# New places for GpSimd's products and TensorE's sums in a selective-scan schedule

## The chip, the core and the metric

The kernel runs on one core of a Trainium2 chip. The metric is the device time in microseconds of one execution. A core has TensorE (PE), VectorE (DVE), ScalarE (ACT), GpSimd (POOL) and SyncE (SP), which here issues the DMAs. Each engine works through its own queue in program order and waits where an instruction needs what another engine has not yet done.

## The reference

Four image-like tensors of 64 x 64 positions and 96 channels pass four layers. Only the first one matters here: a projection to 192 channels, a 3 x 3 convolution, and a selective scan over 4096 positions that is made in four directions (row order and column order, each forward and backward). Cut to the scan:

```python
def step(h, inp):
    u_t, dt_t, B_t, C_t = inp
    dA = jnp.exp(dt_t[..., None] * A)
    h = dA * h + (dt_t * u_t)[..., None] * B_t[:, None, :]
    y = jnp.sum(h * C_t[:, None, :], axis=-1)
    return (h, y)
_, ys = jax.lax.scan(step, h0, (uT, dT, BT, CT))
```

The state has 16 entries a channel. Layer 1 is a convolution, layers 2 and 3 are attention, a Fourier filter and two feed-forward networks with layer norms.

## The kernel before

**Tiles.** 8 channels x 16 states fill the 128 partitions, so the 192 channels make `NG` = 24 groups an image, and the 4 images 96 units. A unit is scanned in two **phases**: an even one in row order ("row") and an odd one in column order ("column"). That makes N = 192 phases. The 4096 positions of a phase are cut into four chunks, q = 0 to 3, of `CH` = 1024.

**Steps.** The loop at L1950 runs 8 steps a phase. Step k = 0 to 3 makes the forward scan of chunk q = k (L1970), which starts from the last column of the chunk before. Step k = 4 to 7 makes the backward scan of chunk q = 7 - k (L1977), which starts from `edge`, the first column of the chunk behind it. VectorE makes all of them. ACT makes the decays exp(dt * A) into PSUM (`decay`, tile `pa`, L1669 and L1675), two PSUM tiles in turn.

**From state to y.** y is the sum over states of h * C. GpSimd multiplies the states by C in place (`times_c`, L1658; C is the tile `rep`), and TensorE sums over the states into the PSUM tile `py` (`reduce`, L1691). Mostly the backward state is added to the forward one first (L1988, VectorE), so that one product serves both. For the chunks in `apart[n]` the backward scan writes over B instead (tile `B` in a row phase, `Bc` in a column one, noted in `gs`), and forward and backward are multiplied and summed each for itself. There is one such chunk, q = 3, while `"pre"` is not in `done`; after that there are two, q = 3 and 2.

**Other work of a phase.** `times_b` (L1653, GpSimd) makes B times dt * u of the next unit in place. `copy_b` (L1628, ACT) copies it into column order for the odd phase. `load_delta`, `load_du` and `load_rep` issue loads on SP. `result` (L1698, ACT) empties `py`, and `store_result` (L1705) issues 16 stores. The forward states lie in five buffers, S0 to S4, that `places` hands out: the scan of chunk 1 takes the buffer of chunk 2 of the phase before, chunk 2 that of chunk 3, chunk 3 that of chunk 1.

**Order.** The scan part runs under a manual schedule, which keeps the order in which the program issues. `plan(n)` enters actions for steps t + k, with t = 8 n, into a table, by `at`. In a step the loop issues first a decay, then the actions of the table, then the scan and what belongs to it, and last `pieces`.

**Side work.** `pieces` fits in what the other layers need: before all scans are fed, the convolution and projections of images 1 to 3 (`before_scans`); then layers 1 to 3 of the images that have been scanned (`rest`). A piece has a cost for each of PE, ACT, POOL, DVE and DMA, in this order. Each step adds the row `gains[step % 16]` to five credits, which are held to `cap`, and pieces run while the credits last. One piece of a convolution block, `LONG`, is allowed only at step 12 of 16. When images 1 to 3 have been through the convolution, `"pre"` is set. What is not done after the last scan is run without shares, and image 3 passes its layers alone in the tail.

Of the kernel before, what the change touches and what calls it, by code (L numbers as in the profile page):

```python
# [73 lines left out]
def layers(ctx: ExitStack, tc: tile.TileContext, a: dict, out):  # L74
# [37 lines left out]
    late = []  # L112
# [22 lines left out]
    done = {}  # L135
# [1446 lines left out]
    def phase(n):  # L1582

        b, g = units[n // 2]
        return b, g, n % 2
# [130 lines left out]
    class Lane:  # L1716
# [32 lines left out]
    credit = [0.0] * 5  # L1749

    gains = [
        (2.8, 1.2, 0.4, 0.8, 1.6), (2.8, 1.2, 0.4, 0.8, 1.6),
        (2.8, 0.2, 0.4, 0.8, 1.6), (2.8, 0.4, 2.2, 0.8, 1.6),
        (2.8, 1.2, 0, 0.8, 1.6), (2.8, 1.4, 0.4, 0.8, 1.6),
        (3.2, 1.0, 1.2, 1, 1.8), (3.2, 2.4, 1.4, 1, 1.8),
        (2.8, 1.4, 0.4, 0.8, 1.6), (2.8, 1.4, 0.4, 0.8, 1.6),
        (2.8, 1.4, 0.4, 0.8, 1.6), (2.8, 2.4, 0.6, 0.8, 1.6),
        (2.8, 2.8, 0.6, 0.8, 1.6), (2.8, 1.4, 0.6, 0.8, 1.6),
        (3.2, 2.4, 0.8, 1, 1.8), (3.2, 2.4, 1.4, 1, 1.8),
    ]  # L1760
    cap = (4.4, 3.0, 3.2, 1.6, 4.0)

    def pieces(step):

        clock[0] += 1
        assert clock[0] % 16 == (step + 1) % 16
        for free, bank in returned:
            free.append(bank)
        returned.clear()
        for e in range(5):  # L1770

            more = 1.25 if e in (2, 4) and clock[0] > 8 * (N - NG) else 1
            credit[e] = min(cap[e], credit[e] + gains[step][e] * more)
        for lane in list(lanes):
            if not lane.live():
                lanes.remove(lane)
                continue
            for s in list(lane.streams):
                while s[1] is not None:
                    if s[1] == NEXT:  # L1780
                        if s[2] == clock[0]:
                            break
                        lane.advance(s)
                        continue
                    if s[1] == LONG:
                        if step != 12:
                            break
                        cost = (0, 5.0, 0, 0)
                    else:
                        cost = s[1]  # L1790
                        if any(
                            c > 0 and credit[e] < min(c, cap[e]) - 0.5 for e, c in enumerate(cost)
                        ):
                            break
                    for e in range(len(cost)):
                        credit[e] -= cost[e]
                    lane.advance(s)
                if s[1] is None:
                    lane.streams.remove(s)
# [88 lines left out]
    def at(step, f, *args):  # L1888
        acts.setdefault(step, []).append((f, args))

    def plan(n):

        t, u = 8 * n, n // 2
        two = "pre" in done
        apart[n] = (3, 2) if two else (3,)
        row = n % 2 == 0
        b, g, _ = phase(n)
        last, first = g == NG - 1, g == 0

        if row:  # L1900
            for q, k in ((0, 7), (1, 8), (2, 9), (3, 10)):
                at(t + k, load_du, u + 1, q)
            for q, k in ((0, 3), (1, 5), (2, 15), (3, 16)):
                at(t + k, load_delta, u + 1, q)
            if last:
                for q in range(NCH):
                    at(t + 2 + q, load_rep, b + 1, 0, q)
                for q, k in ((3, 8), (2, 9), (1, 11), (0, 12)):
                    at(t + k, load_rep, b + 1, 1, q)
            for q, k in ((2, 2), (3, 3), (1, 4), (0, 6)):  # L1910
                at(t + k, copy_b, u, q)
            if first:
                for q in range(NCH):
                    at(t + 6 + q // 2, copy_rep, b, q)
        else:
            for q, k in ((0, 2), (1, 3), (2, 6), (3, 9)):
                at(t + k, times_b, u + 1, q)

        if two:
            at(t + 4, times_c, n, 2)  # L1920
            at(t + 5, times_c, n, 3)
            at(t + 6, times_c, n, 3, True)
            at(t + 7, times_c, n, 2, True)
            at(t + 6, reduce, n, 2)
            at(t + 7, reduce, n, 3)
            at(t + 8, reduce, n, 3, True)
            at(t + 8, reduce, n, 2, True)
        else:
            at(t + 4, times_c, n, 3)
            at(t + 6, times_c, n, 3, True)  # L1930
            at(t + 7, times_c, n, 2)
            at(t + 6, reduce, n, 3)
            at(t + 8, reduce, n, 3, True)
            at(t + 8, reduce, n, 2)
        late = 0 if row else 1
        at(t + 8, times_c, n, 1)
        at(t + 9 + late, times_c, n, 0)
        at(t + 10, reduce, n, 1)
        at(t + 10 + 2 * late, reduce, n, 0)
        if not row:  # L1940
            at(t + 13, result, u)
            for j in range(4):
                at(t + 14 + j, store_result, u, j)

    with tc.manual_schedule():
        ordered[0] = True
# [3 lines left out]
        for step in range(8 * N):  # L1950
            n, k = divmod(step, 8)
            if k == 0:
                plan(n)
                if n % (2 * NG) == 2 * NG - 2 and n // 2 + 1 < len(units):
                    b = units[n // 2 + 1][0]
                    assert done.get(("back", b)) == NBLK, (n, done)
# [10 lines left out]
            if k < 4:  # L1967
                q = k
# [5 lines left out]
            else:  # L1974
                q = 7 - k
# [8 lines left out]
                else:  # L1984
                    if q:
                        edge = big.tile([128, 1], F32, tag="edge", name="edge", bufs=2)
                        nc.vector.tensor_copy(edge, to[:, 0:1])
                    nc.vector.tensor_tensor(Ss[n, q], Ss[n, q], to, ALU.add)  # L1988
            pieces(step % 16)
            if n == N - 1 and k >= 4:  # L1990
                for i in (2 * k - 8, 2 * k - 7):
# [24 lines left out]
def kernel_body(tc: tile.TileContext, a: dict, out):  # L2016
    layers(tc, a, out)
# [117 lines left out]
```

## Time and profile before

| what | value |
|---|---|
| median of three runs | 5528.23 us (5521.36 to 5540.81) |
| the profiled execution, its time | 5537.81 us |
| the profiled execution, its span | 5536.0 us |

Busy time of the engines by stretch, in us:

| stretch, us | length | PE | DVE | ACT | POOL |
|---|---|---|---|---|---|
| 0 to 298, before the scans | 298 | 253 | 94 | 181 | 82 |
| 298 to 1775, one chunk apart | 1477 | 1192 | 1226 | 1101 | 1140 |
| 1775 to 5106, two chunks apart | 3331 | 2464 | 3094 | 2166 | 2710 |
| 5106 to 5536, tail | 430 | 349 | 204 | 118 | 42 |

A row of a group reads: line, engine, operation, out<-in by tile names, shapes and count, then the busy time in all and the mean of one in ns, then the engine's idle time just before them and what ended it. A row of a timeline has the start and the length in us first; "x2" means that two such instructions follow on each other in the row, and brackets hold the idle time before it and what ended it. A row of waits reads: the engine and the instruction that waited, what it waited for, the sum in us, how often, and the longest.

### The profile page before, as it was taken

The numbers are of one execution on the slowest core, as the hardware profiler recorded it, in microseconds if no ns is written. First come the engines' busy times: TensorE is split into PE (matmuls) and PEld (weight loads), VectorE is DVE, ScalarE is ACT, GpSimd is POOL, SyncE is SP. The second block draws the span as 40 slices with busy tenths as digits, with TensorE's granted clock in tenths as the row PEclk, the third lists the DMA queues.
The fourth block names the chain that finished last, engine by engine and source line by source line (L and its number), as shares of the span: only waits on it lengthen the run. The fifth ranks groups of instructions, "written<-read, shape, count | busy, mean of one in ns | idle before, by whom it ended". The sixth has DMA issues, their size and how long they took to land. (4 is left out here: it accounts for less than half of the span.)

```text
span 5536.0 us, 60837 instructions
## 1 busy us (share of the span) xinstructions
PE 4258.0 (77%) x20550; PEld 1581.5 (29%) x20550; DVE 4618.4 (83%) x3098; ACT 3566.0 (64%) x4554; POOL 3973.4 (72%) x1968
## 2 busy tenths in 40 slices
PE   7967888878886876777658876877578767786878
PEld 4422222222221221345102211542012213451346
DVE  4268888788889998999899999999898989998454
ACT  5667777777786568666865677576755676566133
POOL 1357877778778778878887788787987787787000
PEclk9977989888997986678668866787588768886888
DMA  4334444434456533455456434363565335563012
GB/s 125 91 110 115 126 114 117 135 105 124 117 162 175 163 99 89 128 160 156 125 145 173 117 87 119 115 200 103 147 170 146 97 99 165 161 176 96 17 55 96
DMA packets 298092, 694.68 MB, mean 125 GB/s; under 512 B 58184, under 2 KB 95156, under 8 KB 297652
## 3 DMA queue, kind: packets, MB, share of 16 engines
q1 hardware_dynamic: 297780, 690.80, 44.2%
q8 instruction: 162, 2.65, 0.2%
q14 instruction: 150, 1.23, 0.1%
HBM read 564.22 MB, written 126.35 MB: 125 GB/s over the span
## 5 line engine op out<-in xcount | busy, mean ns | idle before, releaser
L1658 POOL TENSOR_TENSOR S<-S,rep 128x1024 f32<-128x1024 f32 x768 | 1806.5, 2362 | 678.9 <-DVE S L1970 628.4
L1691 PE MATMUL py<-S,red 128*32 128x512 f32 x3072 | 956.8, 782 | 380.9 <-POOL S L1658 273.1
L1675 ACT ACTIVATE pa<-dl,nega 128x512 f32<-128x512 f32 x1152 | 792.9, 689 | 579.0 <-DVE Bc L1977 295.3
L1669 ACT ACTIVATE pa<-dl,nega 128x1024 f32<-128x1024 f32 x576 | 642.2, 1115 | 515.7 <-DVE S L1988 239.5
L1653 POOL TENSOR_TENSOR B<-B,rep 128x1024 f32<-128x1024 f32 x384 | 903.0, 2360 | 14.7 <-DMA B<-du_s 14.7
L1970 DVE TENSOR_TENSOR_SCAN S<-pa,S,Bc 128x1024 f32<-128x1024 f32 x288 | 676.3, 2348 | 230.8 <-PE py L1691 161.2
L1970 DVE TENSOR_TENSOR_SCAN S<-pa,S,B 128x1024 f32<-128x1024 f32 x288 | 675.8, 2347 | 134.0 <-PE py L1691 46.3
L1628 ACT COPY Bc<-B 128x1024 f32<-128x1024 f32 x384 | 741.0, 1982 | 0.0
L1988 DVE TENSOR_TENSOR S<-S,pa 128x1024 f32<-128x1024 f32 x439 | 533.7, 1216 | 6.6
L393 PE MATMUL p_conv<-low,conv_w 128*96 128x512 f32 x864 | 421.7, 639 | 32.0 <-ACT u L405 29.4
L1658 POOL TENSOR_TENSOR B<-B,rep 128x1024 f32<-128x1024 f32 x164 | 388.0, 2370 | 75.1 <-DVE pa L1977 38.8
L1977 DVE TENSOR_TENSOR_SCAN B<-pa,B 128x1024 f32<-128x1024 f32 x164 | 379.1, 2312 | 48.2 <-ACT Bc L1628 41.9
L1658 POOL TENSOR_TENSOR Bc<-Bc,rep 128x1024 f32<-128x1024 f32 x165 | 387.0, 2361 | 5.3 <-DVE pa L1977 4.0
L1977 DVE TENSOR_TENSOR_SCAN Bc<-pa,Bc 128x1024 f32<-128x1024 f32 x165 | 381.8, 2314 | 4.7
L1691 PEld LDWEIGHTS py<-S,red 128*32 128x32 f32 x3072 | 118.7, 121 | 908.9 <-POOL S L1658 518.0
L1234 POOL CAST h<-y 128x1536 fp8e5<-128x1536 f16 x64 | 95.5, 1492 | 312.7 <-ACT y L869 301.3
L1977 DVE TENSOR_TENSOR_SCAN pa<-pa,edge,B 128x1024 f32<-128x1024 f32 x124 | 291.5, 2350 | 2.8 <-ACT pa L1669 2.8
L1977 DVE TENSOR_TENSOR_SCAN pa<-pa,edge,Bc 128x1024 f32<-128x1024 f32 x123 | 289.2, 2351 | 5.2 <-ACT pa L1675 5.2
L1691 PE MATMUL py<-Bc,red 128*32 128x512 f32 x660 | 200.0, 787 | 95.1 <-POOL Bc L1658 95.1
L393 PE MATMUL p_conv<-high,conv_w 64*96 64x512 f32 (+1 forms) x576 | 265.0, 597 | 0.0
L1056 PE MATMUL p_mean<-t,centre 96*96 96x512 f32 x256 | 174.3, 792 | 110.7 <-ACT sq L1048 31.8
L1970 DVE TENSOR_TENSOR_SCAN S<-pa,B 128x1024 f32<-128x1024 f32 x96 | 218.9, 2280 | 23.3 <-ACT pa L1669 23.3
(274 smaller groups left out, 7411.4 us busy)
## 6 DMA issues: line engine op xcount, KB each, us to landing
dl<-delta_s SPq DMA_DIRECT2D x770, 256.0 KB
B<-du_s SPq DMA_DIRECT2D x768, 256.0 KB
z_s<-z SPq DMA_DIRECT2D x48, 512.0 KB
zl<-z_s SPq DMA_DIRECT2D x64, 384.0 KB
side<-y_s SPq DMA_DIRECT2D x112, 192.0 KB
rep<-bc_s SPq DMA_DIRECT2D x64, 256.0 KB
tw<-in_dft SPq DMA_DIRECT2D x64, 256.0 KB
side<-in_xT SPq DMA_DIRECT2D x64, 192.0 KB
```

The costliest lines, as they stand in the source:

```text
L393: nc.tensor.matmul(p, lhsT=conv_w[: src.shape[0], k, oc * C : (oc + 1) * C], rhs=src[:, ky : ky + RPB, kx : kx + HW], start=(k == 0), stop ...
L1056: nc.tensor.matmul(pm, lhsT=centre, rhs=t[:, blk(i)], start=True, stop=True)
L1234: nc.gpsimd.tensor_copy(h, y, saturate=False)
L1628: nc.scalar.copy(dst.rearrange("p (w h) -> p h w", h=HW)[:, q * h : (q + 1) * h, :], src.rearrange("p (h w) -> p h w", w=HW),)
L1653: nc.gpsimd.tensor_tensor(Bs[u, q], Bs[u, q], reps[units[u][0], 0, q], ALU.mult)
L1658: nc.gpsimd.tensor_tensor(t, t, c_of(n, q), ALU.mult)
L1669: nc.scalar.activation(pa, dls[u, q // 2][:, at : at + CH], AF.Exp, scale=scale)
L1675: nc.scalar.activation(to[:, k * HW // 2 : (k + 1) * HW // 2, :], src[:, :, q * w : (q + 1) * w], AF.Exp, scale=scale,)
L1691: nc.tensor.matmul(py[32 * j : 32 * j + 32, :], lhsT=red[:, 24 - 8 * s : 56 - 8 * s], rhs=x[:, k * BLK : (k + 1) * BLK], start=s == 0 and ...
L1970: nc.vector.tensor_tensor_scan(s, pas[q], b_of(n, q), Ss[n, q - 1][:, CH - 1 : CH] if q else 0.0, ALU.mult, ALU.add,)
L1977: nc.vector.tensor_tensor_scan(to[:, ::-1], pas[q][:, ::-1], b_of(n, q)[:, ::-1], edge if q < 3 else 0.0, ALU.mult, ALU.add,)
L1988: nc.vector.tensor_tensor(Ss[n, q], Ss[n, q], to, ALU.add)
```

## The change

Three things change in the order and the shares; no instruction is added or removed.

1. `plan` places products, sums, result and stores anew. With two chunks apart, the products stand at t + 3 (forward 2), t + 4 (forward 3), t + 5 (backward 3), t + 6 (backward 2), t + 7 (chunk 1) and t + 8 (chunk 0). With one apart they stand at t + 4 (forward 3), t + 5 (backward 3), t + 6 (2), t + 7 (1) and t + 8 (0). Every sum stands one step behind its product. The result moves from t + 13 to t + 10, the stores with it.
2. `copy_b` takes chunk 3 before chunk 2, and `times_b` of chunks 0 and 1 (and of 2, with one apart) moves one or three steps ahead.
3. `gains` gets other shares for POOL (the third column), and while `"pre"` is not set the gains are multiplied by 0.85 (PE), 0.9 (ACT) and 1.25 (POOL).

```diff
     gains = [
-        (2.8, 1.2, 0.4, 0.8, 1.6), (2.8, 1.2, 0.4, 0.8, 1.6),
-        (2.8, 0.2, 0.4, 0.8, 1.6), (2.8, 0.4, 2.2, 0.8, 1.6),
-        (2.8, 1.2, 0, 0.8, 1.6), (2.8, 1.4, 0.4, 0.8, 1.6),
-        (3.2, 1.0, 1.2, 1, 1.8), (3.2, 2.4, 1.4, 1, 1.8),
-        (2.8, 1.4, 0.4, 0.8, 1.6), (2.8, 1.4, 0.4, 0.8, 1.6),
-        (2.8, 1.4, 0.4, 0.8, 1.6), (2.8, 2.4, 0.6, 0.8, 1.6),
-        (2.8, 2.8, 0.6, 0.8, 1.6), (2.8, 1.4, 0.6, 0.8, 1.6),
-        (3.2, 2.4, 0.8, 1, 1.8), (3.2, 2.4, 1.4, 1, 1.8),
+        (2.8, 1.2, 0, 0.8, 1.6), (2.8, 1.2, 0, 0.8, 1.6),
+        (2.8, 0.2, 2.0, 0.8, 1.6), (2.8, 0.4, 0.6, 0.8, 1.6),
+        (2.8, 1.2, 0.4, 0.8, 1.6), (2.8, 1.4, 0.4, 0.8, 1.6),
+        (3.2, 1.0, 1.2, 1, 1.8), (3.2, 2.4, 1.2, 1, 1.8),
+        (2.8, 1.4, 0.2, 0.8, 1.6), (2.8, 1.4, 0.2, 0.8, 1.6),
+        (2.8, 1.4, 0.2, 0.8, 1.6), (2.8, 2.4, 0.4, 0.8, 1.6),
+        (2.8, 2.8, 0.4, 0.8, 1.6), (2.8, 1.4, 0.4, 0.8, 1.6),
+        (3.2, 2.4, 0.6, 1, 1.8), (3.2, 2.4, 1.2, 1, 1.8),
     ]
...
             more = 1.25 if e in (2, 4) and clock[0] > 8 * (N - NG) else 1
+            if "pre" not in done:
+                more = (0.85, 0.9, 1.25, 1, 1)[e]
             credit[e] = min(cap[e], credit[e] + gains[step][e] * more)
...
-            for q, k in ((2, 2), (3, 3), (1, 4), (0, 6)):
+            for q, k in ((3, 2), (2, 3), (1, 4), (0, 6)):
                 at(t + k, copy_b, u, q)
...
-            for q, k in ((0, 2), (1, 3), (2, 6), (3, 9)):
+            for q, k in ((0, 1), (1, 2), (2, 6 if two else 3), (3, 9)):
                 at(t + k, times_b, u + 1, q)
 
         if two:
-            at(t + 4, times_c, n, 2)
-            at(t + 5, times_c, n, 3)
-            at(t + 6, times_c, n, 3, True)
-            at(t + 7, times_c, n, 2, True)
-            at(t + 6, reduce, n, 2)
-            at(t + 7, reduce, n, 3)
-            at(t + 8, reduce, n, 3, True)
-            at(t + 8, reduce, n, 2, True)
+            order = ((2, False, 3), (3, False, 4), (3, True, 5), (2, True, 6), (1, False, 7))
         else:
-            at(t + 4, times_c, n, 3)
-            at(t + 6, times_c, n, 3, True)
-            at(t + 7, times_c, n, 2)
-            at(t + 6, reduce, n, 3)
-            at(t + 8, reduce, n, 3, True)
-            at(t + 8, reduce, n, 2)
-        late = 0 if row else 1
-        at(t + 8, times_c, n, 1)
-        at(t + 9 + late, times_c, n, 0)
-        at(t + 10, reduce, n, 1)
-        at(t + 10 + 2 * late, reduce, n, 0)
+            order = ((3, False, 4), (3, True, 5), (2, False, 6), (1, False, 7))
+        for q, back, k in (*order, (0, False, 8)):
+            at(t + k, times_c, n, q, back)
+            at(t + k + 1, reduce, n, q, back)
         if not row:
-            at(t + 13, result, u)
+            at(t + 10, result, u)
             for j in range(4):
-                at(t + 14 + j, store_result, u, j)
+                at(t + 11 + j, store_result, u, j)
```

## The prediction

> **What bounds the kernel now.** I read the busy shares first, then VectorE's idle time by cause in each stretch, then single instructions in order of time. The scans (`for step in range(8 * N)`, L1950) run from 298 us to 5106 us; before and behind them lie 298 us and 430 us that the change hardly touches.
>
> ```profile
> PE 4258.0 (77%) x20550; PEld 1581.5 (29%) x20550; DVE 4618.4 (83%) x3098; ACT 3566.0 (64%) x4554; POOL 3973.4 (72%) x1968
> ...
> L1658 POOL TENSOR_TENSOR S<-S,rep 128x1024 f32<-128x1024 f32 x768 | 1806.5, 2362 | 678.9 <-DVE S L1970 628.4
> ...
> L1988 DVE TENSOR_TENSOR S<-S,pa 128x1024 f32<-128x1024 f32 x439 | 533.7, 1216 | 6.6
> ```
>
> VectorE (DVE) is the busiest. The 439 sums of L1988 also tell where the mode switches: an early phase (`"pre"` not done, one chunk apart) makes three, a late one two, and 3 x 55 + 2 x 137 = 439. So 55 phases are early (298 to 1775 us, 26.9 us each) and 137 late (1775 to 5106 us, 24.3 us each). What VectorE waits for in them, first the early stretch, then the late one (us in total, times, longest):
>
> ```profile
> DVE S L1970 <- PE py L1691: 160.4, 37, 7.5
> DVE B L1977 <- ACT Bc L1628: 15.4, 17, 1.1
> ...
> DVE S L1970 <- PE py L1691: 47.1, 30, 4.4
> DVE B L1977 <- ACT Bc L1628: 26.4, 27, 2.6
> ```
>
> So early phases lose 160 us to TensorE sums that free an S buffer late, and late phases lose little: VectorE is busy for 3094 of 3331 us there. Now one late phase, VectorE and then GpSimd (POOL):
>
> ```profile
> 3989.55 2.35 DVE L1970 TENSOR_TENSOR_SCAN S<-pa,S,B 128x1024 f32<-128x1024 f32 x1 [0.30 <-DVE S L1970]
> 3992.20 2.35 DVE L1970 TENSOR_TENSOR_SCAN S<-pa,S,B 128x1024 f32<-128x1024 f32 x1 [0.30 <-DVE S L1970]
> 3994.85 2.35 DVE L1970 TENSOR_TENSOR_SCAN S<-pa,S,B 128x1024 f32<-128x1024 f32 x1 [0.30 <-DVE S L1970]
> ...
> 3991.29 2.34 POOL L1658 TENSOR_TENSOR S<-S,rep 128x1024 f32<-128x1024 f32 x1
> 3997.28 4.66 POOL L1658 TENSOR_TENSOR S<-S,rep 128x1024 f32<-128x1024 f32 x2 [3.65 <-DVE S L1970]
> ```
>
> I call the scan of step k scan k; those shown are 1, 2, 3 (q = 1, 2, 3). The pair of products at 3997.28 is q = 2 and q = 3. S of q = 2 was written by 3994.55 and POOL was free from 3993.63, yet it started at 3997.28, 0.08 after scan 3 ended. The reason is in L1970: scan q starts from `Ss[n, q - 1][:, CH - 1 : CH]`, the last column of the previous S, and the product overwrites that S in place. Backward it is the same (early phase, POOL, then VectorE):
>
> ```profile
> 1398.59 1.27 POOL L578 TENSOR_TENSOR r<-r,lg 96x512 f32<-96x512 f32 x1
> 1400.70 2.35 POOL L1658 TENSOR_TENSOR B<-B,rep 128x1024 f32<-128x1024 f32 x1 [0.85 <-DVE pa L1977]
> ...
> 1395.87 2.29 DVE L1977 TENSOR_TENSOR_SCAN B<-pa,B 128x1024 f32<-128x1024 f32 x1 [0.91 <-ACT Bc L1628]
> 1398.20 2.36 DVE L1977 TENSOR_TENSOR_SCAN pa<-pa,B 128x1024 f32<-128x1024 f32 x1
> ```
>
> B was written by 1398.16 and POOL free at 1399.86, but the product of B waited until the next scan, which only takes its `edge` from B's first column, ended at 1400.56. So the carries are tracked.
>
> **The change, part by part.** *Products.* Inside a step the planned actions come before the scan. Today the product of q = 2 is planned at t + 4, behind scan 3 (t + 3); of backward 3 at t + 6, behind scan 5; of backward 2 at t + 7, behind scan 6. The change plans them at t + 3, t + 5 and t + 6: each stands *in front of* the scan that reads its carry. The product no longer waits for the scan, the scan waits for the product, and takes its carry from the product. In a late phase that is three round trips (scans 3, 5, 6), in an early one a single one (scan 5; its q = 2 product, t + 6, follows the sum it needs). The other products move a step earlier behind operands that are written; they cost nothing.
>
> *Price of a trip.* 0.08 from the scan's end to POOL's start (above), 2.36 the product, 0.04 back: at 2731.70 a scan restarted 0.04 after a product's end. That is 2.48 us. At scan 3 today's gap goes off (0.30 in row phases as shown, some 0.1 in column phases; I take 0.2): 2.28. The sum is 7.24 a late phase, x 137 = **+992**; early 2.48 x 55 = **+136**.
>
> Two rules of the Trainium skill bear on this. "Perfetto Trace Analysis", Identifying the Most-Contended Engine, takes occupancy as a fair measure for Vector and GPSIMD: at 72% POOL would have room, the products' places would be free, and only the removed stalls would count (rival A, 5350). The two rows above speak against it: what counts is who waits for whom, not who is full. "VectorE: DVE Perf Modes", The DRAIN you can't avoid, measured that a semaphore behind each operation costs nothing extra; then scan 3's gap would be 0 and its trip would add 2.48, 27 us more in all. I take the row's gaps.
>
> *What fills the trips.* VectorE's side operations in the late stretch add up to some 264 us (hb, side, t, ln, q, rs_w). They are issued evenly behind the eight scans; those behind scans 2, 4, 5 fall into a trip: 3/8 is 99 at best, 0 at worst. I take **-80**.
>
> *Stalls that go.* Late waits of VectorE on others are some 170 us (PE 47, Bc copy 26, exponentials 35, the rest small). With 7 us more in each phase the other engines get ahead; I take **-110** (-60 to -170). The Bc copies are also reordered, q = 3 first, whose B is overwritten first. Early: the sums for q = 2 and for backward 3 leave TensorE's queue one and two steps sooner, and the phase has 2.48 us more; of 160 + 15, **-155** (-90 to -175).
>
> *POOL's queue in front of a trip.* Its side operations (casts, sums, rs_y) are 165 us busy in the late stretch and wait 134 us for ACT, TensorE and VectorE. One that stands before a product of a trip now holds VectorE. Ahead of q = 2 POOL has two or three products (4.7 to 7.1 us) for three scans (7.6 us), so most side work fits; behind scans 4 and 5 it doesn't. 0 if all fits, 299 if all counts; a fifth: **+60**. `times_b` of q = 3 now stands behind the q = 0 product; scan 3 waits for the q = 2 product behind both anyway: 0. `times_b` 0 and 1 come a step sooner after their loads (waits on B's DMA are 4.8 us in the late stretch): in the range.
>
> *TensorE's sums one step behind.* They wait for POOL more, and behind them stand side matmuls, ACT's evacuations and the exponentials. Below nothing if buffers come free sooner; at most today's 35 us of exponential waits again. VectorE now waits for POOL itself and TensorE follows POOL by one sum (1.05 us): 0. *Result and stores*, three steps sooner: the ys copy and 16 SP issues, behind which the next delta and du loads stand. Delta loads are made more than a phase ahead: 0; if that cover failed, a step, 3 us, a pair.
>
> *Shares.* POOL's side share falls from 12.0 to 9.4 per 16 steps; early, PE's from 46.4 to 39.4, ACT's from 24.6 to 22.1, POOL's to 11.75. A convolution block needs by the code's own costs about 32, 21 and 10, and starts its `LONG` piece only at one step in 16, so it still gets one pair, with ACT tight. Some pairs may be missed. Each phase that stays early costs 26.5 instead of 30.6: none to ten, I take five: **-20**. The last image's feed-forward ends later by POOL's share, but from 5106 to 5120 us TensorE is busy for 3.8 us only, before the reload of y: 0 to +20, **+5**.
>
> **Sum**, against the profiled execution (span 5536.0, time 5537.8): late 992 - 80 - 110 + 60 = +862; early 136 - 155 = -19; -20; +5: +828, so 6366. The profiled execution lies 10 above the median of the three runs (5528.2); taking that off and rounding, **6350 us**. A late phase would take 24.3 + 6.3 = 30.6 us. Its own bounds: fills -99 to 0, late stalls -170 to -60, queue 0 to +200, early stalls -175 to -90, shares 0 to -40; not all at one end: 6200 to 6500.
>
> **Rivals.** *A, the trips aren't there* (the wait on the next scan is some other wait, and the carry isn't tied to the product). Then stalls go: about 110 of 160 early and 70 late: 5528 - 180, 5350. For it: the 160 us are real, POOL is idle 28%. Against: two products that wait for just the scan that reads their carry, 0.08 and 0.14 behind its end. 6%. *B, POOL's queue decides*: side operations and what they wait for all land in trips, from the point where POOL reaches the q = 2 product later than scan 2 ends. All 299 instead of 60: 6590. Against it is the smaller share. 13%. *C, only the forward carry is tied* (edge lies in another tile): late 137 x 2.28 = 312, fills 33, queue 20, no early trip: 312 - 33 - 110 + 20 - 155 + 5 = +39, about 5570, with some 60 to either side. Against it the B product above. 4%. *D, trips well filled*: every term at its low end (fills -19, late stalls -60, queue -60, early stalls -20, and 15 phases more instead of 5, -40): 6150. 7%. The forecast has 70%.
>
> Low 6140 takes in D, high 6580 half of B; A and C stay out. A measurement of this kernel tells a difference of 0.3% (17 us): faster 0.07 (A and the low end of C), same 0.01 (of C), slower 0.92.
>
> **What would show it.** VectorE's waits for POOL S, B and Bc (L1658's place), near zero now, should be the largest: about 137 x 3 + 55 times 2.2 to 2.5 us, some 1000 us. Late phases 30 to 31 us, early 26 to 27 with the wait on PE py under 40 us. VectorE's busy share falls to 72 to 73%. A late phase of 24 us, or waits of VectorE on POOL under 200 us, would prove me wrong; 32 us or more with side operations before the products is B.

## The result, and the profile after

The changed kernel takes 6521.98 us (median of four runs, 6516.73 to 6526.7), against 5528.83 us for the kernel before (four runs): a ratio of 1.1794, with an interval of 1.1771 to 1.1817. It is slower by 993 us. The profiled execution has a span of 6521.9 us, 986 more than that of before. From here on all sums are made between these two spans.

The page of after, first its busy shares and then three rows of its groups. In a row the last part is the idle time of the engine just before these instructions, and what ended it:

```profile
PE 4731.1 (73%) x20542; PEld 1667.7 (26%) x20542; DVE 4628.5 (71%) x3099; ACT 3577.3 (55%) x4557; POOL 3982.7 (61%) x1966
...
L1658 POOL TENSOR_TENSOR S<-S,rep 128x1024 f32<-128x1024 f32 x768 | 1807.9, 2354 | 1551.3 <-DVE S L1976 868.3
...
L1965 DVE TENSOR_TENSOR_SCAN pa<-pa,Bc 128x1024 f32<-128x1024 f32 x96 | 226.3, 2358 | 280.9 <-POOL Bc L1658 264.8
...
L1976 DVE TENSOR_TENSOR S<-S,pa 128x1024 f32<-128x1024 f32 x441 | 536.1, 1216 | 6.6
```

VectorE and GpSimd do what they did: 4628.5 and 3982.7 us busy, 10 and 9 us more than before, and the product of an S takes 2.354 us instead of 2.362. But both are idle more. GpSimd's idle time before these products rose from 679 to 1551 us, and nearly all of it ends with an operation of VectorE. VectorE in turn stands before its scans (the row of the backward one has 281 us) until GpSimd ends a product. Two engines, neither above 71%, wait for each other in turn. The 441 sums of L1976 are 3 x 57 + 2 x 135, so 57 phases are early now, not 55.

By stretch (length; then busy us and number of instructions of PE, PEld, DVE, ACT and POOL; then the granted clock, the DMA share and GB/s), early phases first:

```profile
296.00:1920.00 1624.00, 1335.24 (x3136) 369.05 (x3136) 1273.57 (x752) 1129.58 (x1422) 1174.41 (x617) 0.85 0.41 120
1920.00:6088.00 4168.00, 2796.55 (x13333) 975.50 (x13331) 3056.30 (x1807) 2148.74 (x2667) 2686.28 (x1231) 0.69 0.37 106
```

Before, the two lengths were 1477 and 3331 us. From the starts of the scans a late phase takes 30.87 us instead of 24.31, an early one 28.50 instead of 26.84. VectorE's 3056 us of 4168 in the late stretch leave 1112 idle, where 237 were. What it waited for there (us in total, times, longest):

```profile
DVE S L1958 <- POOL S L1658: 352.0, 120, 7.3
DVE B L1965 <- POOL B L1658: 158.1, 64, 4.3
DVE Bc L1965 <- POOL Bc L1658: 157.6, 66, 4.7
DVE pa L1965 <- POOL B L1658: 157.5, 66, 2.9
DVE pa L1965 <- POOL Bc L1658: 149.6, 61, 6.5
```

The first row is scan 3, the next two are scan 5, the last two scan 6: 975 us for GpSimd's products. The kernel before has 2 us of them in its late stretch, all in one row:

```profile
DVE S L1970 <- POOL S L1658: 1.6, 6, 0.3
```

All other waits that the view of after puts to a cause are 100 us (191 before). But 57 of these 100 us are trips too: 22 waits before scans 3, 5 and 6 end 0.03 us after a product, though the view puts them down to something else. This row, for instance, holds two scans 3 that start 0.03 us after the product of the S that they take their carry from:

```profile
DVE S L1958 <- DMA yT_s<-ys: 11.5, 2, 5.8
```

So late phases have 1032 us of waits for products and 43 of others. The early stretch, the same view:

```profile
DVE pa L1965 <- POOL Bc L1658: 115.3, 28, 9.6
DVE pa L1965 <- POOL B L1658: 74.6, 29, 4.8
DVE S L1958 <- ACT pa L1675: 60.3, 23, 6.8
DVE B L1965 <- ACT Bc L1628: 27.9, 12, 4.8
DVE S L1958 <- ACT pa L1669: 27.5, 5, 23.4
DVE S L1958 <- PE py L1691: 15.5, 11, 5.5
```

Here the products cost 196 us with the small rows (3 before), and the others 161 (257 before). The wait for TensorE's sums did go, from 160.4 to 15.5, but exponentials (ACT pa) and the Bc copy have 116 us in the rows shown, where the same rows had 48. So the 986 us are: +1223 waits for products (1030 late, 193 early), -244 other waits (-148 and -96), +10 busy time of VectorE. That is 989; the 3 us too many are shorter gaps, rounding and the two ends.

One late phase in order of time, VectorE and then GpSimd:

```profile
4699.86 4.83 DVE L1958 TENSOR_TENSOR_SCAN S<-pa,S,Bc 128x1024 f32<-128x1024 f32 x2
4707.21 2.35 DVE L1958 TENSOR_TENSOR_SCAN S<-pa,S,Bc 128x1024 f32<-128x1024 f32 x1 [2.52 <-POOL S L1658]
4709.60 2.29 DVE L1965 TENSOR_TENSOR_SCAN Bc<-pa,Bc 128x1024 f32<-128x1024 f32 x1
4714.35 2.35 DVE L1965 TENSOR_TENSOR_SCAN Bc<-pa,Bc 128x1024 f32<-128x1024 f32 x1 [2.46 <-POOL Bc L1658]
4719.15 2.36 DVE L1965 TENSOR_TENSOR_SCAN pa<-pa,Bc 128x1024 f32<-128x1024 f32 x1 [2.45 <-POOL Bc L1658]
```

```profile
4704.84 2.34 POOL L1658 TENSOR_TENSOR S<-S,rep 128x1024 f32<-128x1024 f32 x1 [0.26 <-DVE S L1958]
4709.64 2.34 POOL L1658 TENSOR_TENSOR S<-S,rep 128x1024 f32<-128x1024 f32 x1 [2.46 <-DVE S L1958]
4711.97 2.35 POOL L1658 TENSOR_TENSOR Bc<-Bc,rep 128x1024 f32<-128x1024 f32 x1
...
4716.78 2.34 POOL L1658 TENSOR_TENSOR Bc<-Bc,rep 128x1024 f32<-128x1024 f32 x1 [0.15 <-DVE Bc L1965]
```

Read them across. Scan 2 ends at 4704.69; GpSimd multiplies its S from 4704.84 to 4707.18; scan 3, which takes its carry from that S, starts at 4707.21, 0.03 later. Scan 4 needs no carry and follows at once. Then comes the product of its Bc and scan 5, and once more for scan 6: three round trips of about 2.5 us in one phase.

Over all late phases VectorE's mean idle time right before scan 5 is 2.37 us (column) and 2.40 (row), before scan 6 it is 2.44 and 2.38, and before scan 3 it is 2.95 and 2.75. From the end of scan 2 to the start of scan 3 it is 2.55 us in the median and 3.16 in the mean. The mean is longer because GpSimd first ends something else in some phases: 0.39 us between the end of scan 2 and the product, 0.20 before the one for scan 5 and 0.09 before the one for scan 6. That is its queue in front of the trips, 0.68 us a phase, 92 us in all.

### The profile page after: what moved, and what is told of

It reads as the page before. It is cut to its first block, busy times and chain, and to the rows that moved or that the text cites. A ratio compares the mean times of both kernels' runs of the same rounds, so it can differ in the third digit from the quotient of the medians.

```text
span 6521.9 us, 60446 instructions
## 1 busy us (share of the span) xinstructions
PE 4731.1 (73%) x20542; PEld 1667.7 (26%) x20542; DVE 4628.5 (71%) x3099; ACT 3577.3 (55%) x4557; POOL 3982.7 (61%) x1966
## 3 DMA queue, kind: packets, MB, share of 16 engines
q8 instruction: 162, 2.65, 0.2%
## 5 line engine op out<-in xcount | busy, mean ns | idle before, releaser
L1691 PE MATMUL py<-S,red 128*32 128x512 f32 x3072 | 1155.0, 839 | 946.4 <-POOL S L1658 945.2
L1669 ACT ACTIVATE pa<-dl,nega 128x1024 f32<-128x1024 f32 x576 | 643.0, 1117 | 991.4 <-DVE S L1976 479.4
L1976 DVE TENSOR_TENSOR S<-S,pa 128x1024 f32<-128x1024 f32 x441 | 536.1, 1216 | 6.6
L1965 DVE TENSOR_TENSOR_SCAN pa<-pa,Bc 128x1024 f32<-128x1024 f32 x96 | 226.3, 2358 | 280.9 <-POOL Bc L1658 264.8
L1658 POOL TENSOR_TENSOR Bc<-Bc,rep 128x1024 f32<-128x1024 f32 x164 | 386.0, 2354 | 22.5 <-DVE Bc L1965 19.1
L1965 DVE TENSOR_TENSOR_SCAN pa<-pa,B 128x1024 f32<-128x1024 f32 x96 | 226.3, 2358 | 233.9 <-POOL B L1658 232.0
L1691 PE MATMUL py<-Bc,red 128*32 128x512 f32 x656 | 235.8, 803 | 110.4 <-POOL Bc L1658 110.2
L1691 PE MATMUL py<-B,red 128*32 128x512 f32 x652 | 226.1, 781 | 101.4 <-POOL B L1658 101.4
```

What stands on the lines that cost most here:

```text
L1658: nc.gpsimd.tensor_tensor(t, t, c_of(n, q), ALU.mult)
L1669: nc.scalar.activation(pa, dls[u, q // 2][:, at : at + CH], AF.Exp, scale=scale)
L1691: nc.tensor.matmul(py[32 * j : 32 * j + 32, :], lhsT=red[:, 24 - 8 * s : 56 - 8 * s], rhs=x[:, k * BLK : (k + 1) * BLK], start=s == 0 and ...
L1965: nc.vector.tensor_tensor_scan(to[:, ::-1], pas[q][:, ::-1], b_of(n, q)[:, ::-1], edge if q < 3 else 0.0, ALU.mult, ALU.add,)
```

## The experiments

Each time stands with the ratio to the kernel before on the same chip, whose medians there were 5532 to 5535 us. A *trip* is a scan that waits for the product of the tile it takes its carry from.

**The trips alone taken out.** The change, but the three products behind the scan that needs their carry:

```diff
-order = ((2, False, 3), (3, False, 4), (3, True, 5), (2, True, 6), (1, False, 7))
+order = ((2, False, 4), (3, False, 4), (3, True, 6), (2, True, 7), (1, False, 7))
-order = ((3, False, 4), (3, True, 5), (2, False, 6), (1, False, 7))
+order = ((3, False, 4), (3, True, 6), (2, False, 6), (1, False, 7))
```

> The changed kernel, but the three products whose carry a later scan reads stand behind that scan again: late mode forward 2 at t + 4, backward 3 at t + 6, backward 2 at t + 7; early mode backward 3 at t + 6. Everything else stays as changed (sums one step behind, shares, copies). Trip theory: the whole loss sits in these places, so VectorE's waits for GpSimd's products fall from some 1170 us to under 100 and the time to 5350 to 5560 us. Rival (queue theory: the tighter sums and the smaller shares make the loss): it stays above 6200 us. If part of the early loss (28.5 us a phase) comes from TensorE and ScalarE lagging, early phases stay above 26 us.

Measured: 5605.88 us, 1.0131 (1.0116 to 1.0146). So the trips are worth 6522 - 5606 = 916 us, 2.44 in an early phase (28.50 - 26.06) and 5.91 in a late one (30.87 - 24.96). Waits for products are down to 6 us, so the theory of the trips holds. But the time is 46 us above the expected range: what is left of the change is no gain, it costs 74 us. I call this kernel *the one without trips*. VectorE's waits in this kernel's early stretch:

```profile
DVE S L1958 <- ACT pa L1675: 65.5, 29, 7.1
DVE pa L1965 <- ACT pa L1675: 45.8, 14, 4.4
...
DVE S L1958 <- PE py L1691: 25.3, 12, 5.5
```

TensorE's sums no longer hold VectorE, and ACT's exponentials do: early phases are 26.06 us, 0.78 better than before and not the 2.8 better that the prediction's 155 us would have brought. Late phases are 24.96, 0.65 worse, nearly all of it in row phases (25.73 against 24.54; column 24.20 against 24.09). There VectorE's wait for TensorE's sums fell from 47 to 3 us, but that for exponentials rose from 44 to 107, and its layer-norm operations wait 63 us for TensorE (`p_rstd`) instead of 13.

**One trip alone put in.** The kernel before, with one number changed:

```diff
-at(t + 4, times_c, n, 2)
+at(t + 3, times_c, n, 2)
```

> The kernel before, with one edit: the late product of forward chunk 2 moves from t + 4 to t + 3, in front of the scan that takes its carry from it; its sum stays at t + 6. Trip theory: one trip of 2.48 us less today's gap of 0.2 in 137 phases is +312 us, less what side operations fill and stalls that go: 5730 to 5850 us, with some 2.3 to 3.2 us of wait before scan 3. Rival (the carry is not tied to the product): 5510 to 5550 us. If GpSimd's queue often stands in front of this product, above 5900 us.

Measured: 5851.16 us, 1.0577 (1.0561 to 1.0593), so 319 us for the forward trip, at the upper edge of the range. Nearly all of it is in late phases, which take 26.56 us (137 x 2.25 = 308); early ones stay at 26.82. The row of VectorE's waits that is new, over the whole span:

```profile
DVE S L1970 <- POOL S L1658: 381.1, 116, 9.9
```

**The same places, without the tie.** The change as it is, but scans 3, 5 and 6 take their carry from a copied column. The product may then overwrite the tile whenever it likes:

```diff
+carry = big.tile([128, 1], F32, tag="carry", name="carry", bufs=2)
+nc.vector.tensor_copy(carry, s[:, CH - 1 : CH])
...
-edge = to[:, 0:1]
+edge = big.tile([128, 1], F32, tag="edge", name="edge", bufs=2)
+nc.vector.tensor_copy(edge, to[:, 0:1])
```

> The changed kernel with the products at the same early places, but each carry is copied into a column of its own by VectorE directly behind the scan that makes it, and the next scan starts from the copy (three copies of some 0.16 us a late phase, one an early one). Trip theory: the scan no longer waits for the product: 5400 to 5620 us, of which the copies cost 137 x 3 x (0.16 to 0.4) = 66 to 165 us. Rival (the early places as such slow the kernel, through GpSimd's queue and TensorE's sums): above 6000 us.

Measured: 5634.12 us, 1.0182 (1.0165 to 1.0199). The products stand as early as in the change, and 888 us are gone; the waits of late scans for products fall to 7 us. It is the carry's tie to the overwritten tile that costs, not the early place. The time is 14 us above the expected range and 28 above the kernel without trips. The added copies keep VectorE busy for about 71 us (462 of 0.15 us), so what the early places would bring without them stays open.

**The shares alone.** The kernel before with the new `gains` and the factors (0.85, 0.9, 1.25, 1, 1).

> The kernel before with the new shares alone (the new column for POOL, and the factors 0.85, 0.9 and 1.25 in the early stretch); all places as before. Trip theory: the shares are next to nothing of the loss: 5490 to 5570 us, and the early stretch lasts 57 phases instead of 55. Rival (the shares starve the side work, which makes the early stretch long and the tail late): 5650 us or more.

Measured: 5528.0 us, 0.9991 (0.9982 to 0.9999), as expected, and with 57 early phases instead of 55 (its trace has 441 of the sums, as after). So the two more early phases of the change come from the shares, and the shares are worth nothing that matters.

**Sums two steps behind.** What do the 74 us come from? The kernel without trips, with TensorE's sums a step later, and the result with them:

```diff
-at(t + k + 1, reduce, n, q, back)
+at(t + k + 2, reduce, n, q, back)
-at(t + 10, result, u)
+at(t + 11, result, u)
```

> As e1_behind (products whose carry is read later stand behind that scan), with every sum two steps behind its product instead of one, and the result one step later. Theory S (the sums close behind their products make TensorE stand waiting for GpSimd in front of side matmuls, whose evacuations hold the exponentials back): of e1_behind's 74 us over the kernel before most goes, 5530 to 5560 us, and TensorE's wait on products of S in the late stretch falls from 428 us to under 250. Theory Q (the place of times_b 3 behind the product of chunk 0 does it): no change from 5606, 5590 to 5620 us. It would rise above 5620 if the later sums bring the wait for S buffers back.

Measured: 5582.79 us, 1.0091 (1.0077 to 1.0104). That lies between the two ranges. Late phases improve from 24.96 to 24.62, and TensorE's wait for products of S in the late stretch falls from 438 to 242 us, VectorE's for exponentials from 107 to 77. Early ones worsen to 26.76, and the old wait is back (early stretch):

```profile
DVE S L1958 <- PE py L1691: 113.0, 29, 10.4
```

So the distance of the sums shifts the stall between two places: close behind, TensorE waits for GpSimd and holds up what follows on TensorE and ACT; further behind, the S buffer comes free late. It gives back 0.34 of the 0.65 us that late phases had lost.

**The last `times_b` in front.** In the change the product of B for q = 3 comes a step behind that of chunk 0. This is the kernel without trips with both in step t + 8, where the table has `times_b` first:

```diff
-for q, k in ((0, 1), (1, 2), (2, 6 if two else 3), (3, 9)):
+for q, k in ((0, 1), (1, 2), (2, 6 if two else 3), (3, 8)):
```

> As e1_behind, with times_b of chunk 3 planned one step earlier, so that it stands in front of chunk 0's product as in the kernel before. Theory Q: row phases, which e1_behind made 25.73 instead of 24.54 us in the late stretch, come back, 67 x 1.2 = 80 us less: 5525 to 5550 us. Theory S: only the 28 us of VectorE's wait on B go at most: 5575 to 5610 us.

Measured: 5671.17 us, 1.0249 (1.0235 to 1.0263). Neither theory holds: this is 65 us worse, not better. Row phases of the late stretch go to 26.96 us, and in that stretch the copy of B into column order is now what VectorE waits for most, 63.9 us where the kernel without trips has 10.7. Why row phases suffer was not found.

**The order of the Bc copies alone.** The kernel before with one line of the change:

```diff
-for q, k in ((2, 2), (3, 3), (1, 4), (0, 6)):
+for q, k in ((3, 2), (2, 3), (1, 4), (0, 6)):
```

> The kernel before with the new order of the Bc copies alone (chunk 3 before chunk 2). The wait of the backward scan on the Bc copy (15 us early, 26 us late) goes: 5488 to 5510 us. Rival (another wait is next, the copy of chunk 3 stands behind times_b 3): 5520 to 5535 us.

Measured: 5539.27 us, 1.0012 (1.0004 to 1.002). That is above both ranges, and no gain. In the late stretch the wait of the backward scans for Bc fell from 26.4 to 6.1 us, and their wait for the exponentials of L1669 rose from 7.4 to 21.7. Why these exponentials became late is not shown: a copy of B stands right before them on ACT in only 3 of the 21 waits.

**Shares, copies and an earlier chunk 2 in early phases.** The kernel with the new shares, the copies in the new order, and in an early phase chunk 2's product at t + 6 and its sum at t + 7.

> The kernel before with the new shares, the new order of the Bc copies, and in the early mode the product and the sum of chunk 2 one step earlier (t + 6 and t + 7), ahead of that step's side matmuls; the sums are otherwise where they were. If the early wait for an S buffer (160 us before) can go without another taking its place: 5400 to 5450 us. If TensorE's lag then shows as late exponentials, as in e1_behind: 5480 to 5520 us.

Measured: 5587.69 us, 1.0097 (1.0081 to 1.0112). Both ranges were missed. VectorE still waits 164.4 us for TensorE's sums in early phases. To move one sum does not remove that stall, and what makes this kernel 55 us slower than the one before was not followed up.

**The early trip alone.** The kernel without trips, with the change's own plan for early phases:

```diff
-order = ((3, False, 4), (3, True, 6), (2, False, 6), (1, False, 7))
+order = ((3, False, 4), (3, True, 5), (2, False, 6), (1, False, 7))
```

> As e1_behind, but in the early mode backward 3 stands at t + 5 again, in front of the scan that takes its edge: the early trip alone. 57 phases x 2.48 us = +141 over e1_behind's 5606: 5720 to 5760 us, early phases 28.5 us as in the changed kernel, late ones 24.9 to 25.0. If the trip covers waits that e1_behind has anyhow, less: 5660 to 5720.

Measured: 5731.6 us, 1.0352 (1.0338 to 1.0366), 126 us above the kernel without trips and in the expected range, and early phases of 28.44 us: 2.38 x 57 = 136. Its waits for backward products are the change's to the microsecond (115.9 + 74.6 = 190.5), so some 60 us of them take the place of other waits.

**The two backward trips alone.** The kernel before with

```diff
-at(t + 6, times_c, n, 3, True)
-at(t + 7, times_c, n, 2, True)
+at(t + 5, times_c, n, 3, True)
+at(t + 6, times_c, n, 2, True)
```

> The kernel before with the two late backward products in front of the scans that take their edge (backward 3 at t + 5, backward 2 at t + 6), sums as before: two trips in 137 phases. Trip theory with the prediction's price: 2 x 2.48 x 137 = 680, less fills of 66 and stalls that go: 5980 to 6160 us. If a trip takes in waits that come anyhow, as the changed kernel against e1_behind suggests (5.9 us for three): 2 x 2.0 x 137 = 548, about 6080. Rival (edge lies in another tile, so nothing waits): 5520 to 5540.

Measured: 6438.61 us, 1.1628 (1.161 to 1.1646), 904 us for two trips. That is well above what was expected, and as much as the three trips of the change cost in its late phases (5.91 x 135 = 798 against the kernel without trips, 886 against the one before). VectorE and then GpSimd, one late phase:

```profile
4637.08 2.29 DVE L1977 TENSOR_TENSOR_SCAN Bc<-pa,Bc 128x1024 f32<-128x1024 f32 x1
4644.12 2.35 DVE L1977 TENSOR_TENSOR_SCAN Bc<-pa,Bc 128x1024 f32<-128x1024 f32 x1 [4.74 <-POOL Bc L1658]
```

```profile
4637.13 4.65 POOL L1658 TENSOR_TENSOR S<-S,rep 128x1024 f32<-128x1024 f32 x2 [2.69 <-DVE S L1970]
4641.74 2.34 POOL L1658 TENSOR_TENSOR Bc<-Bc,rep 128x1024 f32<-128x1024 f32 x1
```

The forward product of chunk 2 still waits for scan 3. So GpSimd has two forward products and the one of Bc to make, in a row, from 4637.13 to 4644.08, while VectorE has only scan 4 of 2.29 us to put beside them: scan 5 waits 4.74 us and not 2.48, and so it does over all late phases (4.7 on the mean). In the change one of the two forward products is made during the stop at scan 3, and scan 5 finds a shorter queue (0.20 us on the mean, here 2.65). Trips do not add up one by one; what stands in front of the product on its engine counts.

**The early plan without its trip, the late plan as before.** Early phases as in the kernel without trips, late phases as in the kernel before, the copies in the new order; once with the new shares and once with the old ones.

> Early phases planned as in e1_behind (26.06 us each there), late phases planned as in the kernel before (24.31), with the new shares and the new order of the copies. If the two modes keep their times: 57 x 26.06 instead of 55 x 26.84 + 2 x 24.31, so 40 us less than before: 5480 to 5505 us. If the early lateness of TensorE is handed on: 5520 to 5550.

> As h1_hybrid with the old shares and without the factors of the early stretch. If the lower shares of TensorE are what lets the early sums close behind their products pay, the early phases are 26.5 us or more: 5510 to 5550. If the shares don't matter, as h1_hybrid: 5480 to 5505.

Measured: 5526.29 us, 0.9988 (0.9978 to 0.9998), with the new shares, and **5512.11 us, 0.9959 (0.9946 to 0.9971)**, with the old ones. The second is 0.4% below the kernel before and 15.5% below the change. Its early phases take 26.14 us instead of 26.84, its late ones 24.44 instead of 24.31: 55 x 0.70 - 137 x 0.13 = 21, and 22.5 were measured against the median of before. Both are short of the 40 us that were expected, in the main because the late phases got 0.13 us longer though they are planned as before; why they did was not followed up. Of the 14 us between the two some 10 lie in the tail (441 us with the new shares, 431 with the old).

## Why the prediction was right, and where its terms were off

The sum was +828 on the span; +986 was measured. The mechanism is the one that was named: the trips come and go with the place of the product and with the carry's tie. But the time lies above the 6200 to 6500 us that the prediction's own terms allowed, and inside its range only because the upper end was stretched half way to rival B, which is not what happened. So that it lies in the range is in part luck. Most of the missing 158 us lie in the early phases, which were forecast at 26 to 27 us: 57 x 28.50 against 55 x 26.84 and two late phases of 24.31 is +99, where the terms for early phases and shares gave -39. Late phases gave 135 x (30.87 - 24.31) = +886, against +862.

- **The price of a trip, right.** 2.48 us was reckoned; the phase shown has 2.45 to 2.52, and the means right before scans 5 and 6 are 2.37 to 2.44. What makes today's gap of 0.30 us before scan 3 in row phases is not shown; it is not the carry as such, since scan 5 takes one from scan 4 and follows it after 0.04 us (1398.16 to 1398.20 in the lines of before).
- **Late trips, their fill and the queue** (992 - 80 + 60 = 972): +1030 us of waits for products were measured. Of the difference 0.2 x 135 = 27 us are the gap at scan 3 that the prediction took off and the waits hold, and some 30 are the queue: 92 us by GpSimd's own instructions, not 60. VectorE's side operations between these scans are 0.65 us a phase, 88 us, close to the 80.
- **Late stalls that go** (-110): -148, of which the rows by cause show only 91. The room for it comes from the trips alone. With them taken out, the rest of the change makes late phases 0.65 us longer; the trips hid that cost, which the prediction had at about nothing.
- **Early trips** (+136): +193 us of waits. This is a mis-sized term. The prediction reckoned with GpSimd's queue only in late phases and had none in front of the early trip. One column phase, GpSimd's row of instructions:

```profile
672.86 4.65 POOL L1653 TENSOR_TENSOR B<-B,rep 128x1024 f32<-128x1024 f32 x2
677.48 2.33 POOL L1658 TENSOR_TENSOR S<-S,rep 128x1024 f32<-128x1024 f32 x1
679.78 1.25 POOL L584 TENSOR_TENSOR u<-r,u 96x512 f32<-96x512 f32 x1
681.00 2.34 POOL L1658 TENSOR_TENSOR Bc<-Bc,rep 128x1024 f32<-128x1024 f32 x1
```

  Scan 4 had ended at 676.42; `times_b`, the forward product and a side operation came first, and scan 5 started at 683.37, after 6.96 us. Over all early phases the mean before scan 5 is 4.12 us in column phases (28) and 2.57 in row phases (29): 28 x (4.12 - 2.48) = 46 of the 57 us. In column phases GpSimd first ends, on the mean, 0.88 us of the forward product, 0.75 of side operations and 0.16 of `times_b`. Row phases have no `times_b` and hardly anything in front (0.2 us); that the earlier `times_b` pushed the rest into the trip is likely, but no run moved them alone.
- **Early stalls** (-155): the term that was furthest off. The wait for TensorE's sums fell by 145 us, as forecast, but all waits other than for products, this one among them, fell by only 96. Without the trip, the first experiment gained 55 x 0.78 = 43 us. The prediction had asked what would be late next in late phases, and not here. Exponentials are: 71 us in the early stretch of after, 147 in that of the kernel without trips, 38 before. One stretch of ACT and VectorE, early:

```profile
1346.91 0.68 ACT L405 ACTIVATE u<-p_conv,conv_b 96x512 f32<-96x512 f32 x1 [6.90 <-PE p_conv L393]
1347.49 1.40 ACT L1675 ACTIVATE pa<-dl,nega 128x512 f32<-128x512 f32 x2
...
1348.98 2.35 DVE L1958 TENSOR_TENSOR_SCAN S<-pa,S,Bc 128x1024 f32<-128x1024 f32 x1 [3.56 <-ACT pa L1675]
```

  ACT stands 6.90 us before a bias of the convolution that TensorE has not finished, the exponentials are queued behind it, and the scan waits 3.56 us for them. TensorE's lag reaches VectorE by another road.
- **Shares** (-20, five more early phases): two more, for no gain: an early phase at 28.50 saves 2.4 us against a late one, some 5 in all. (GpSimd's old shares add up to 11.6 and not to 12.0, and D's 15 more early phases go beyond the bound of ten; nothing hangs on either.) **Tail** (+5): 434 us instead of 430.

Of the rivals, A (no trips) and C (the backward edge not tied) would have shown no waits of VectorE for products of B and Bc; the four rows of the late stretch sum to 623 us. B (all side work lands in trips) came near in its time, 6590, but is not the reason: it needed 299 us of queue in late phases, where 92 were found, and scans 5 and 6 wait for less than a plain trip. D (every term at its low end, 6150) is 370 us off.

What stays open: the other half of the 0.65 us that the rest of the change costs in late phases, and why the last `times_b` in front of chunk 0's product makes it worse.

## What to carry to other kernels

Before an in-place operation is moved forward, list every later instruction that reads any part of its tile, a single carry column too: each of them becomes a round trip between two engines, and no share of busy time shows that beforehand. Price a trip as hand-over, operation and hand-over, and add what stands ahead of it in that engine's queue, in each mode of the schedule for itself. When a stall is to go, look for the engine that its cause holds up next.

## What the runs showed of the hardware

Hand-overs between VectorE and GpSimd are small beside the work: in the late phase shown 0.08 us from scan 3's end to GpSimd's start, 0.15 from scan 2's, and 0.03 back. GpSimd's products took the same time whether VectorE stood still (2.34 us at 4704.84) or was scanning (2.34 at 4709.64).

TensorE was granted a lower clock in the kernels whose late phases have trips. In the late stretch it was 0.73 with the forward trip alone, 0.69 after and 0.68 with the two backward trips alone, where TensorE stood idle for 1128, 1371 and 1577 us, against 0.76 before and 0.78 with the trips taken out, where it stood idle for 867 and 920. Its busy time rose with the lower clock, from 4258 us before to 4731 after for nearly the same matmuls. It did not set the end of a phase here: in the late stretch of after VectorE waited 3.4 us for its sums. The first experiment took the trips away and the clock came back, so it followed them. That agrees with the Trainium skill ("TensorE: Matmul & The Clock Gate", Part 1: The HAM clock gate), which has the clock set by how busy TensorE has been just before.
